# Planned order for SyncE and GpSimd, and a new place for the bf16 parts of the local minima

## Chip, core and metric

One core of a Trainium2 chip runs the kernel. The metric is the device time of one execution in microseconds (us), as the median of several. Engines are named as in the profile: PE is the matrix engine (TensorE) and PEld its weight loads, DVE is VectorE, ACT is ScalarE, POOL is GpSimd, SP is SyncE. SP computes nothing here; it issues nearly all transfers (DMAs), one after the other, and each issue first waits for the semaphores of its source and its destination.

## The reference

From one input x of 4096 rows by 256, two branches are computed on the same layer-normed rows and added to x. The attention branch has 16 heads of 16, whose softmax runs over a rational function of the scores; its projections divide a squared product by a squared distance. The FFN branch is a stack of two layers, each with a local attention (windows of 128 rows that look at themselves and at the window before, 8 heads of 64) and an MLP with a gated GELU of width 682.

```python
def yat_attention(xn, ...):               # S = 4096, H = 16, Dh = 16
    q, k, v = yat_dense(xn, wq, bq, aq), yat_dense(xn, wk, bk, ak), yat_dense(xn, wv, bv, av)
    attn = einsum('bqhd,bkhd->bhqk', q, k)
    sq = attn * attn
    w = sq / (qn + kn - 2.0 * sq + EPS)   # qn, kn: squared norms of q and k
    return softmax(w) @ v @ wo + bo

def layer(x, ...):                        # twice, over all 4096 rows
    q, k, v = split(shift_token(x) @ wqkv)
    q, k = rotary(l2norm(q) * qs, l2norm(k) * ksc)
    x = x + local_attention(q, k, v) @ wo # softmax over 256 keys, with a mask
    a, g = split(layernorm(shift_token(x)) * lg + lb) @ w1 + b1)
    return x + (a * gelu(g)) @ w2 + b2

out = x + yat_attention(layernorm(x)) + layer(layer(layernorm(x)))
```

## The kernel before

A prologue of some 260 us norms the rows, makes q, k and v and stores them in device memory, q and k as three bf16 parts each. Then the main part begins, in which two streams of work are woven into each other.

**The large attention** is cut into 512 tiles: for each of the 16 heads, 32 blocks of 128 queries against all 4096 keys. A tile has two halves of 2048 keys. Per half, PE makes the scores (line L951), ACT squares them (L955), DVE subtracts (`less`, L959). Then a tile is done in one of two ways. Unpaired, each half goes by itself through `positive` (DVE, L972), `log` and `power` (ACT, L978 and L981). Paired, DVE multiplies both halves (`product`, L963), one half goes through the three, and `signed` (DVE, L985) finishes it: less work for ACT, more for DVE. Then `weights` (DVE, L993, twice per tile) makes the softmax's argument and its maximum per query, in `mm`, of which an accumulator read writes the last column. `maximum` (L998 to L1007) turns the maximum of 128 queries into a row of three bf16 parts, `mrow`: SP sends the first part with a DMA (L1004), POOL subtracts it from the maximum (L1007), SP sends the second, POOL subtracts again, SP sends the third. `turn` (PE) first multiplies -1 with that row (L1014), which puts the negated maximum into the bank, and adds the transposed weights (L1017); `exp` (ACT, L1025) and `values` (PE, L1036) follow. After every fourth tile `copied` takes the sum out (ACT, L1043, into `ob`) and SP stores it (L1045).

**The FFN chain** is one long list of steps, written as a generator that yields a step (engine, cost in ns) ahead of each piece of code. Per block of 256 rows and layer (32 in all) it makes q, k, v, and four times `looked` and `summed` (heads in pairs). `looked` makes the scores on PE and the masked, scaled scores with their minimum on DVE (L740, four times, minima in `mx`). Then come the minimum's three bf16 parts: four operations on POOL (L745 to L748, 128x4 each) and three DMAs (L751) into a row `frow`. `summed` uses the row as `turn` does (L760), from a due time of 10,000 ns after the step in which `looked` ended. Then come the MLP of the layer, in 8 blocks of 512 rows (L813 to L915), and `finals`, which adds the attention's result, head half by head half, to the output: `front` (nine DMAs, L1082, L1083, L1087), `middle` (DVE L1095 to L1102; a store `rec` L1097 and a load `pT` L1099 that reads it back), `back` (PE L1108 and L1115, DVE L1110 and L1120). The last block of rows is closed by `last_rows` (L1146 to L1156), after everything else.

**What sets the order.** A planner runs through both streams while the program is built. It keeps one list of ready tasks for PE, ACT, DVE and one called X, which takes no engine; it picks by rank, charges each task its cost, and writes the instructions when a task starts. A task X with no cost is thus a point in planned time, behind the step ahead of it. The chain's steps get a due time in half tiles, from the costs so far (DVE's and ACT's times 0.5, PE's times 1) over the constant CHAIN_NS = 2.5755e6. Whether a tile is paired is decided by which of ACT and DVE has more planned load. For PE, ACT and DVE this planned order is kept as it is; for SP and POOL, a scheduler of the framework decides the order of instructions, from its own estimates and priorities. Every engine works through its list in order, so an instruction that waits holds up all behind it.

Of the kernel before, what the change touches and what calls it, by code (L numbers as in the profile page):

```python
# [182 lines left out]
def plan_all(plan, acts, chain, halves):  # L183
# [32 lines left out]
    def soft(n, m):  # L216
        i, half = divmod(n, 2)
        exps = []
        for z in range(2):
            w = plan.add("PE", 427 + 8 * 109, lambda z=z: acts.turn(n, z), n + RANK["W"] + 0.3 * z, [m], [last["W"]],  # L220
                         takes=[(PS, (n, z, 1))], gives=[(R, n)] if z else [])
            last["W"] = w
            e = plan.add("ACT", 905, lambda z=z: acts.exp(n, z), n + RANK["E"] + 0.3 * z, [w], takes=[(PE2, (n, z))], gives=[(PS, (n, z, 1))])
            exps.append(e)
        fresh = [last["copy"]] if half == 0 and i % 4 == 0 else []
        last["P"] = plan.add("PE", 874, lambda: acts.values(n), n + RANK["P"], exps + fresh, [last["P"]],
                             gives=[(PE2, (n, 0)), (PE2, (n, 1))], mode="C")
        if half and i % 4 == 3:
            last["copy"] = plan.add("ACT", 465, lambda: acts.copied(i), n + RANK["O"], [last["P"]])

# [42 lines left out]
def tile_yat_attention_and_local_ffn(ctx: ExitStack, tc: tile.TileContext, io, out):  # L273
# [322 lines left out]
    def ffn():  # L596
        for l in range(DEPTH):
# [63 lines left out]
            for g in range(NGF):  # L661
# [50 lines left out]
                if g + 1 < NGF:  # L712
                    nxt = fetch(g + 1)
                osum = fa.tile([128, 2, INNER], F32, name="xm2")

                def looked(c):

                    P = fb.tile([128, 2, 2, 256], F32, name="P")
                    mx = fb.tile([128, 4], F32, name="mx")
# [16 lines left out]
                    yield step("DVE", 1620, give=2)  # L736
                    for e in range(2):
                        for b in range(2):
                            mk = msk[:, 0 if (g == 0 and b == 0) else 1]
                            V.tensor_tensor_reduce(P[:, e, b], pss[:, e, b], mk, rn[:, 0, b, 2 * c + e:2 * c + e + 1], 3.0e38,  # L740
                                                   ALU.add, ALU.min, mx[:, 2 * e + b:2 * e + b + 1])
                    yield step("X", 0)
                    m3 = fb.tile([128, 3, 4], BF, name="fm3")
                    md = fb.tile([128, 4], F32, name="fmd")
                    G.tensor_copy(m3[:, 0], mx)  # L745
                    G.tensor_tensor(m3[:, 1], mx, m3[:, 0], ALU.subtract)
                    G.tensor_tensor(md, mx, m3[:, 0], ALU.subtract)
                    G.tensor_tensor(m3[:, 2], md, m3[:, 1], ALU.subtract)  # L748
# [3 lines left out]
                    held[c] = P, mT, plan.now + 10000.0  # L752
# [30 lines left out]
                for c in range(5):  # L783
                    if c < 4:
                        yield from looked(c)
                    if c:
# [17 lines left out]
                V.tensor_tensor(xm, pw, xres, ALU.add)  # L804
                nc.sync.dma_start(xm_d[l][g * GT + 1:(g + 1) * GT + 1].rearrange("(t p) c -> p t c", p=128), xm)
# [23 lines left out]
            for g in range(NG):  # L829
# [16 lines left out]
                if g + 1 < NG:  # L846
                    nxt = shifted(g + 1)
                h2 = []
                for c in range(2):
# [6 lines left out]
                    V.tensor_scalar(h2[c], ph, lngb[:, 0, c:c + 1], lngb[:, 1, c:c + 1], ALU.mult, ALU.add)  # L856
                gg = fa.tile([128, 6, 512], F32, name="kv")
# [38 lines left out]
                if l < DEPTH - 1:  # L896
                    for c in range(2):
# [6 lines left out]
                        V.tensor_copy(xoT, ph)  # L904
                        for z in range(2):
# [3 lines left out]
                else:  # L909
# [4 lines left out]
                    V.tensor_tensor(xo, xo, xin, ALU.add)  # L914
                    nc.sync.dma_start(ff_d[g].rearrange("(t p) c -> p t c", p=128), xo)  # L915
# [7 lines left out]
    class Acts:  # L923
# [11 lines left out]
        def scores(self, n, z):  # L935
            i, half = divmod(n, 2)
            h, qt = tiles[i]
            if half == 0 and z == 0:
# [4 lines left out]
                if qt % 4 == 0 and i // 4 + 1 < len(quads):  # L943
# [96 lines left out]
        def copied(self, i):  # L1040
            h, qt = tiles[i]
            self.ob = hp.tile([128, 512], F32, name="ob", bufs=1)
            A.copy(self.ob, pav)  # L1043
            if i + 1 < len(tiles):
# [120 lines left out]
    with tc.manual_schedule(engines={mybir.EngineType.PE, mybir.EngineType.Activation, mybir.EngineType.DVE}):  # L1165
# [59 lines left out]
```

## Time and profile before

| what | value |
|---|---|
| median of 3 runs | 7330.53 us (7329.86 to 7334.82) |
| the profiled execution | 7328.83 us, its span 7327.0 us |
| granted TensorE clock, mean | 0.981 |
| rows of maxima: POOL L1007, 1024 times | 1033.9 us busy, 1010 ns each |
| parts of the local minima: POOL L745 to L748, 128 times each | 216.9, 203.2, 200.9 and 152.2 us |
| DMA issues of `mrow`, `frow`, Q, `ob` | 1536, 384, 384, 127 |

The span is the time from the first to the last instruction of the profiled execution. "Busy" counts an engine's own instructions; issuing a DMA and waiting are not busy time. A line such as "PE pt L1014 <- DMA mrow<-mm: 108.2, 38, 8.8" reads: PE stood idle ahead of L1014 until a DMA into mrow landed, 108.2 us in all, 38 times, 8.8 at most. In rows of groups the numbers after the bar are busy us and mean ns of one. Rows of a timeline give start, duration, engine, line, operation and tiles, the count, and in brackets the idle time before and what ended it.

### The profile page before, as it was taken

The numbers are of one execution on the slowest core, as the hardware profiler recorded it, in microseconds if no ns is written. First come the engines' busy times: TensorE is split into PE (matmuls) and PEld (weight loads), VectorE is DVE, ScalarE is ACT, GpSimd is POOL, SyncE is SP. The second block draws the span as 40 slices with busy tenths as digits, with TensorE's granted clock in tenths as the row PEclk, the third lists the DMA queues.
The fourth block names the chain that finished last, engine by engine and source line by source line (L and its number), as shares of the span: only waits on it lengthen the run. The fifth ranks groups of instructions, "written<-read, shape, count | busy, mean of one in ns | idle before, by whom it ended". The sixth has DMA issues, their size and how long they took to land. (4 is left out here: it accounts for less than half of the span.)

```text
span 7327.0 us, 158565 instructions
## 1 busy us (share of the span) xinstructions
PE 6747.6 (92%) x66274; PEld 4786.4 (65%) x67136; DVE 6907.5 (94%) x7307; ACT 6972.8 (95%) x6761; POOL 1806.4 (25%) x1567
## 2 busy tenths in 40 slices
PE   7799999999999998899999999999999999999998
PEld 3466666666676665666666676666666666666665
DVE  8999999999999998899999999999999999899998
ACT  8899999999999998899999999999999999899998
POOL 0123233223332322212223322332232220011210
PEclk9899999999999999999999999999999999999999
DMA  3201010010000111011110010101010023101012
GB/s 130 76 16 21 17 24 15 17 22 17 20 19 15 30 40 26 19 31 24 35 21 19 20 19 17 23 14 25 15 23 15 17 59 87 36 21 31 20 46 77
DMA packets 542303, 223.84 MB, mean 31 GB/s; under 512 B 374988, under 2 KB 514003, under 8 KB 539538
## 3 DMA queue, kind: packets, MB, share of 16 engines
q1 hardware_dynamic: 539650, 212.73, 12.3%
q8 instruction: 527, 8.63, 0.5%
q14 instruction: 190, 1.56, 0.1%
q10 hardware_dynamic: 1936, 0.92, 0.0%
HBM read 124.59 MB, written 88.08 MB: 29 GB/s over the span
## 5 line engine op out<-in xcount | busy, mean ns | idle before, releaser
L1017 PE MATMUL pt<-ident,r 128*128 128x128 f32 x16384 | 2497.5, 276 | 0.0
L1017 PEld LDWEIGHTS pt<-ident,r 128*128 128x128 f32 x16384 | 2082.7, 143 | 577.3 <-issue 199.4
L1025 ACT ACTIVATE pe<-pt 128x1024 f32<-128x1024 f32 x2048 | 2178.8, 1099 | 147.0 <-PE pt L1017 122.5
L955 ACT ACTIVATE r<-pt 128x1024 f32<-128x1024 f32 x2048 | 2120.9, 1104 | 86.5 <-PE pt L951 45.0
L1007 POOL TENSOR_TENSOR mm<-mm 128x1 f32<-128x1 f32 x1024 | 1033.9, 1010 | 4714.3 <-DVE mm L993 4547.7
L1014 PE MATMUL pt<-mrow,neg 128*128 128x512 bf16 x4096 | 1577.6, 385 | 220.8 <-DMA mrow<-mm 108.2
L978 ACT ACTIVATE u<-u 128x2048 f32<-128x2048 f32 x702 | 1395.4, 1997 | 26.8 <-DVE u L972 26.4
L981 ACT ACTIVATE u<-u 128x2048 f32<-128x2048 f32 x702 | 1403.5, 1999 | 0.7
L959 DVE TENSOR_SCALAR r<-r 128x2048 f32<-128x2048 f32 x1024 | 1242.5, 1221 | 65.2 <-ACT r L955 64.8
L993 DVE CUSTOM_DVE_ANT_0 r<-r,u,mm 128x2048 f32<-128x2048 f32 x512 | 1201.3, 2346 | 63.4 <-ACT u L981 58.4
L951 PE MATMUL pt<-K,Q 128*128 128x512 bf16 x3234 | 1013.2, 383 | 199.7 <-ACT pe L1025 129.8
L993 DVE CUSTOM_DVE_ANT_0 r<-r,u 128x2048 f32<-128x2048 f32 x512 | 1169.1, 2283 | 13.0 <-ACT u L981 6.4
L1036 PE MATMUL pv<-pe,vh 128*17 128x128 f32 x32768 | 1074.1, 275 | 21.4 <-ACT ob L1043 7.9
L1036 PEld LDWEIGHTS pv<-pe,vh 128*17 128x17 f32 x32768 | 819.0, 97 | 298.7 <-issue 279.7
L985 DVE SCALAR_TENSOR_TENSOR u<-u 128x2048 f32<-128x2048 f32 x322 | 736.1, 2286 | 74.6 <-ACT u L981 73.8
L951 PEld LDWEIGHTS <-Q 128*128 128x128 bf16 x4096 | 375.4, 99 | 574.6 <-issue 393.6
L963 DVE TENSOR_TENSOR u<-r,r 128x2048 f32<-128x2048 f32 x322 | 735.6, 2285 | 1.9
L1014 PEld LDWEIGHTS <-neg 128*128 128x128 bf16 x4096 | 406.7, 99 | 350.7 <-issue 249.6
L972 DVE TENSOR_SCALAR u<-r 128x2048 int32<-128x2048 int32 x380 | 457.1, 1219 | 1.6 <-DMA q_d<-pb 1.5
L972 DVE TENSOR_SCALAR u<-u 128x2048 int32<-128x2048 int32 x322 | 394.4, 1225 | 7.5
L863 PE MATMUL pf<-pT,wqkv_s 128*128 128x512 f32 (+1 forms) x768 | 367.5, 601 | 4.2 <-DVE kv L883 1.5
L745 POOL CAST fm<-mx 128x4 bf16<-128x4 f32 x128 | 216.9, 1695 | 481.2 <-DVE mx L740 470.5
(211 smaller groups left out, 6005.1 us busy)
## 6 DMA issues: line engine op xcount, KB each, us to landing
o<-ob SPq DMA_DIRECT2D x127, 256.0 KB
mrow<-mm SPq DMA_DIRECT2D x1536, 0.2 KB
Q<-q_d SPq DMA_DIRECT2D x256, 48.0 KB
K<-k_d SPq DMA_DIRECT2D x32, 384.0 KB
tab<-in_tables_dram SPq DMA_DIRECT2D x32, 256.0 KB
xres<-xres SPq DMA_DIRECT2D x32, 256.0 KB
xm<-xm SPq DMA_DIRECT2D x32, 256.0 KB
P<-xm SPq DMA_DIRECT2D x32, 256.0 KB
```

The source lines that it names most:

```text
L951: T.matmul(ps[:, j * 512:(j + 1) * 512], lhsT=Q[:, (qt % 4) * 128:(qt % 4 + 1) * 128], rhs=K[:, o + j * 512:o + (j + 1) * 512], start=True ...
L955: A.activation(self.r[n][:, z * 1024:z * 1024 + 1024], self.pt.pop((n, z)), AF.Square)
L959: V.tensor_scalar(self.r[n], self.r[n], 1.0, 1.0e-9, ALU.subtract, ALU.subtract)
L972: V.tensor_scalar(self.part(i, h).bitcast(I32), src.bitcast(I32), 0x7FFFFFFF, None, ALU.bitwise_and)
L978: A.activation(self.part(i, h), self.part(i, h), AF.Ln)
L981: A.activation(self.part(i, h), self.part(i, h), AF.Exp, scale=-2.0)
L993: V.tensor_tensor_reduce(self.r[2 * i + h], self.r[2 * i + h], self.part(i, h), 1.0 if self.paired[i] else -0.5, init, ALU.mult, ALU.max, ...
L1007: G.tensor_tensor(mm[:, c_ + 1:c_ + 2], mm[:, c_:c_ + 1], head[:, 2 * c_ + 1:2 * c_ + 2], ALU.subtract)
L1014: T.matmul(pt[:, 512 * b:512 * b + 512].rearrange("p (s n) -> p s n", s=4), lhsT=neg1, rhs=self.mT[i].unsqueeze(1).broadcast_to([128, 4, 1 ...
L1017: T.matmul(pt[:, 512 * b + j * 128:512 * b + (j + 1) * 128], lhsT=self.r[n][:, o + j * 128:o + (j + 1) * 128], rhs=ident, is_transpose=Tru ...
L1025: A.activation(pe, self.pt.pop((n, z)), AF.Exp)
L1036: T.matmul(pav[32 * (j % 4):32 * (j % 4) + 17, (qt % 4) * 128:(qt % 4) * 128 + 128], lhsT=vh[h % 2][:, kt, :], rhs=pe[:, j * 128:(j + 1) * ...
```

## The change

SP and POOL are added to the engines whose order is the planned one. So that a DMA stands on SP's list behind the planned end of what it reads, X steps are put ahead of several stores, the store of `ob` becomes an X task of its own behind the copy (`stored`), the loads of the next block (`fetch`, `shifted`) move behind later steps, and Q is loaded at the second tile of a quad instead of the first. The three parts of a local minimum are made by three instructions on DVE in the step that makes the minima (cost 2050 instead of 1620): two subtractions of the upper half of the number's bits, seen as bf16, and one cast of all three parts. The local rows' due time is 6,000 ns instead of 10,000. The rows of maxima stay as they were, with POOL's two subtractions.

```diff
--- before.py
+++ after.py
@@ -227,6 +227,7 @@
                              gives=[(PE2, (n, 0)), (PE2, (n, 1))], mode="C")
         if half and i % 4 == 3:
             last["copy"] = plan.add("ACT", 465, lambda: acts.copied(i), n + RANK["O"], [last["P"]])
+            plan.add("X", 0, lambda: acts.stored(i), n, [last["copy"]])
 
     def begin(n):
         sq = []
@@ -709,14 +710,12 @@
                                  start=k == 0, stop=k == 1)
                     yield step("DVE", 600, give=True)
                     V.tensor_copy(va[:, (2 * g + b) % 3, :, 0:FD], pv.rearrange("p (h d) -> p h d", h=FH))
-                if g + 1 < NGF:
-                    nxt = fetch(g + 1)
                 osum = fa.tile([128, 2, INNER], F32, name="xm2")
 
                 def looked(c):
 
                     P = fb.tile([128, 2, 2, 256], F32, name="P")
-                    mx = fb.tile([128, 4], F32, name="mx")
+                    mx = fb.tile([128, 3, 4], F32, name="mx")
 
                     yield step("PE", 1200, "R", take=2)
                     pss = ps_s.tile([128, 2, 2, 256], F32, name=acts.name("pt", "f"))
@@ -733,23 +732,22 @@
                                 else:
                                     T.matmul(pss[:, e, b, j * 128:(j + 1) * 128], lhsT=lq, rhs=kT[r:r + 64, c, (s0, s1)[j]],
                                              start=True, stop=True)
-                    yield step("DVE", 1620, give=2)
+                    yield step("DVE", 2050, give=2)
                     for e in range(2):
                         for b in range(2):
                             mk = msk[:, 0 if (g == 0 and b == 0) else 1]
                             V.tensor_tensor_reduce(P[:, e, b], pss[:, e, b], mk, rn[:, 0, b, 2 * c + e:2 * c + e + 1], 3.0e38,
-                                                   ALU.add, ALU.min, mx[:, 2 * e + b:2 * e + b + 1])
+                                                   ALU.add, ALU.min, mx[:, 0, 2 * e + b:2 * e + b + 1])
+                    m3 = fb.tile([128, 3, 4], BF, name="fm3")
+                    hd = mx.bitcast(BF).rearrange("p j (n w) -> p j n w", w=2)[:, :, :, 1]
+                    for c_ in range(2):
+                        V.tensor_tensor(mx[:, c_ + 1], mx[:, c_], hd[:, c_], ALU.subtract)
+                    V.tensor_copy(m3, hd)
                     yield step("X", 0)
-                    m3 = fb.tile([128, 3, 4], BF, name="fm3")
-                    md = fb.tile([128, 4], F32, name="fmd")
-                    G.tensor_copy(m3[:, 0], mx)
-                    G.tensor_tensor(m3[:, 1], mx, m3[:, 0], ALU.subtract)
-                    G.tensor_tensor(md, mx, m3[:, 0], ALU.subtract)
-                    G.tensor_tensor(m3[:, 2], md, m3[:, 1], ALU.subtract)
                     mT = frow[c % 2]
                     for c_ in range(3):
                         nc.sync.dma_start(mT[c_:c_ + 1], m3[:, c_])
-                    held[c] = P, mT, plan.now + 10000.0
+                    held[c] = P, mT, plan.now + 6000.0
 
                 def summed(c):
                     P, mT, at = held.pop(c)
@@ -783,6 +781,8 @@
                 for c in range(5):
                     if c < 4:
                         yield from looked(c)
+                    if c == 1 and g + 1 < NGF:
+                        nxt = fetch(g + 1)
                     if c:
                         yield from summed(c - 1)
                 oT = fa.tile([128, 4, GT], F32, name="qT")
@@ -802,6 +802,7 @@
                 yield step("DVE", 600, give=True)
                 xm = fa.tile([128, 2, D], F32, name="xm")
                 V.tensor_tensor(xm, pw, xres, ALU.add)
+                yield step("X", 0)
                 nc.sync.dma_start(xm_d[l][g * GT + 1:(g + 1) * GT + 1].rearrange("(t p) c -> p t c", p=128), xm)
 
             if l == DEPTH - 1:
@@ -843,8 +844,6 @@
                 hn = fa.tile([128, 4, D], F32, name="qT")
                 for t in range(4):
                     V.tensor_scalar(hn[:, t], xh[:, t], mv[:, t, 0:1], rstd[:, t:t + 1], ALU.subtract, ALU.mult)
-                if g + 1 < NG:
-                    nxt = shifted(g + 1)
                 h2 = []
                 for c in range(2):
                     yield step("PE", 510, take=True)
@@ -854,6 +853,8 @@
                     yield step("DVE", 725, give=True)
                     h2.append(fb.tile([128, 512], F32, name="pT"))
                     V.tensor_scalar(h2[c], ph, lngb[:, 0, c:c + 1], lngb[:, 1, c:c + 1], ALU.mult, ALU.add)
+                if g + 1 < NG:
+                    nxt = shifted(g + 1)
                 gg = fa.tile([128, 6, 512], F32, name="kv")
 
                 def up(s_, m):
@@ -902,6 +903,7 @@
                         yield step("DVE", 600, give=True)
                         xoT = fb.tile([128, 512], F32, name="pT")
                         V.tensor_copy(xoT, ph)
+                        yield step("X", 0)
                         for z in range(2):
                             nc.sync.dma_start(xT_d[l + 1][2 * g + z][c * 128:(c + 1) * 128], xoT[:, z * GT:(z + 1) * GT])
                     for z in range(2):
@@ -912,6 +914,7 @@
                     nc.sync.dma_start(xin, acc_d[g].rearrange("(t p) c -> p t c", p=128))
                     yield step("DVE", 1135)
                     V.tensor_tensor(xo, xo, xin, ALU.add)
+                    yield step("X", 0)
                     nc.sync.dma_start(ff_d[g].rearrange("(t p) c -> p t c", p=128), xo)
 
 
@@ -940,7 +943,7 @@
                     assert self.valued >= 8 * NT * h
                     load_k(h + 1)
                     load_v(h + 1)
-                if qt % 4 == 0 and i // 4 + 1 < len(quads):
+                if qt % 4 == 1 and i // 4 + 1 < len(quads):
                     load_q(*quads[i // 4 + 1])
             if z == 0:
                 self.r[n] = hr.tile([128, 2048], F32, name=self.name("r", n))
@@ -1041,6 +1044,9 @@
             h, qt = tiles[i]
             self.ob = hp.tile([128, 512], F32, name="ob", bufs=1)
             A.copy(self.ob, pav)
+
+        def stored(self, i):
+            h, qt = tiles[i]
             if i + 1 < len(tiles):
                 nc.sync.dma_start(o_d[qt // 4][h], self.ob)
                 if h == H - 1:
@@ -1162,7 +1168,7 @@
 
     plan = Plan()
     acts = Acts()
-    with tc.manual_schedule(engines={mybir.EngineType.PE, mybir.EngineType.Activation, mybir.EngineType.DVE}):
+    with tc.manual_schedule(engines={mybir.EngineType.PE, mybir.EngineType.Activation, mybir.EngineType.DVE, mybir.EngineType.SP, mybir.EngineType.Pool}):
         plan_all(plan, acts, chain(), 2 * len(tiles))
         last_rows(acts.ob)
```

## The prediction

> **What bounds the kernel now.** I read the page first: part 1 for the load of each engine, then the waits, then busy time by stretches of 200 us, then the timeline around one stall and around the end.
>
> ```profile
> span 7327.0 us, 158565 instructions
> PE 6747.6 (92%) x66274; PEld 4786.4 (65%) x67136; DVE 6907.5 (94%) x7307; ACT 6972.8 (95%) x6761; POOL 1806.4 (25%) x1567
> ```
>
> Three engines are nearly full. What is left to gain is idle time of ACT, 7327.0 - 6972.8 = 354 us, and of DVE, 420 us. The second view shows where ACT's idle time lies:
>
> ```profile
> 800.00:1000.00 200.00, 190.41 (x1991) 140.38 (x2012) 195.97 (x228) 198.64 (x197) 70.67 (x62) 1.00 0.08 15
> 1000.00:1200.00 200.00, 185.26 (x1884) 136.26 (x1906) 187.74 (x196) 190.45 (x192) 46.70 (x44) 0.98 0.12 24
> sum 4400.00, PE 4117.56 PEld 3028.53 DVE 4245.33 ACT 4312.75 POOL 1271.97; mean PE 187.16 PEld 137.66 DVE 192.97 ACT 196.03 POOL 57.82
> ```
>
> The columns after the stretch are PE, PEld, DVE, ACT and POOL busy. The sum is over 22 stretches, 400 to 2600 and 3800 to 6000 us, in which the FFN's local attention runs beside the large attention. ACT is idle for 4400.00 - 4312.75 = 87 us there, very unevenly: 1.4 us in a quiet stretch, 9.6 in the next one. The eleven quietest of the 22 lose 1.5 us each. At that rate all would lose 33, so 54 us are stalls. The waits name them:
>
> ```profile
> PE pt L1014 <- DMA mrow<-mm: 108.2, 38, 8.8
> PEld L1014 <- DMA mrow<-mm: 44.7, 15, 9.3
> ACT pe L1025 <- PE pt L1017: 122.5, 105, 9.9
> ```
>
> PE waits 153 us for the row of maxima, and ACT then waits for PE. Asked by stretch, 33.7 of the 153 fall between 400 and 2600 us and 30.9 between 3720 and 6000; 52.5 lie from 2600 to 3720, in the FFN's MLP. One stall in order of time, first POOL's rows, then SP's and PE's:
>
> ```profile
> 1126.93 2.24 POOL L745 CAST fm<-mx 128x4 bf16<-128x4 f32 x1 [10.67 <-DVE mx L740]
> 1129.25 1.08 POOL L746 TENSOR_TENSOR fm<-mx,fm 128x4 bf16<-128x4 f32 x1
> 1130.29 2.25 POOL L747 TENSOR_TENSOR fmd<-mx,fm 128x4 f32<-128x4 f32 x1
> 1132.61 1.06 POOL L748 TENSOR_TENSOR fm<-fmd,fm 128x4 bf16<-128x4 f32 x1
> 1133.62 3.39 POOL L1007 TENSOR_TENSOR mm<-mm 128x1 f32<-128x1 f32 x2
> ...
> 1129.20 4.96 SPq L751 DMA_DIRECT2D frow<-fm  x3
> 1134.26 3.24 SPq L1004 DMA_DIRECT2D mrow<-mm  x3
> 1140.22 0.59 PE L1014 MATMUL pt<-mrow,neg 128*128 128x512 bf16 x1 [3.53 <-DMA mrow<-mm]
> ```
>
> The maximum was ready at 1129.13 (the end of its read on DVE at 1129.05). Its row was sent at 1134.26, since POOL was still on the four operations for the local minima and SP stood in front of their transfers. PE lost 3.5 us. So in the attention stretches a good part of the 54 us comes from what the change removes.
>
> **The change, part by part.** *POOL's four operations per local tile go* (L745 to L748, 128 times; means 1.695, 1.587, 1.570 and 1.189 us, 6.04 together). POOL then has only the 1024 subtractions of L1007. Upper bound of the gain: all 54 us of stalls, with SP's order below. Lower bound: 0, if the rows stay late for another reason. L1007 alone runs from 189 to 11197 ns, and its longest lie in the MLP, which this part does not touch. I take 54 in the attention stretches and nothing in the MLP's 52.5.
>
> The trace first: 6.04 us for four operations of 128x4 on POOL stand against 0.155 us for one such operation on DVE (L402, median), ten times as long for each. The Trainium skill (GPSIMD Engine Reference, Key points) says that for elementwise work the DVE is structurally about 2x faster. By that rule the four would hold POOL for 1.2 us, a fifth of what is measured, the gain would be about 11 us, and the sum below would come out some 43 us later, slower than before. The trace decides here.
>
> *DVE gets three tiny operations per local tile*: two subtractions of 128x4 (0.155 each, row L402) and a cast of 128x12, which the trace has not; the nearest are 0.166 (L404, 128x4) and 0.169 (L703, 128x16), from below 0.081 (the read of an accumulator). 128 x (2 x 0.155 + 0.166) = 61 us, bounds 31 and 65.
>
> *The planner answers.* It charges DVE 430 ns more per local tile and so picks fewer paired tiles. In the built programs 316 tiles of 512 are paired instead of 322. Each of the six takes 2.286 + 2.285 + 1.225 - 2 x 1.219 = 3.36 us from DVE and gives ACT one Ln and one Exp of 128x2048, whose starts lie 1.80 us apart when they follow each other (2880.09 and 2881.89). So DVE: 61 - 20 = +41 us; ACT: 12 x 1.80 = +22 us. ACT is the fuller engine (196.03 against 192.97 of 200 in the stretches above), and DVE's 7 us idle in each 200, some 3.5%, cover its 41 us (0.6%). I take 22; without that cover it is 22 + 41 = 63.
>
> *SP and POOL in the planned order.* In front of the rows, SP now waits for many things:
>
> ```profile
> SPq L751 <- POOL fm L745: 433.7, 116, 15.0
> SPq L1045 <- ACT ob L1043: 249.0, 67, 10.1
> SPq L338 <- PE pt L951: 227.6, 62, 11.2
> SPq L638 <- DVE qr L647: 103.3, 23, 9.8
> ```
>
> The change moves each of these behind the event that frees it: Q by one tile, the fetch of hT and tab behind two local blocks, `ob` behind its copy, the local minima's transfers behind DVE. Their gain is inside the 54. What strict order adds: in the final rows, `rec` and `pT` now stand together, so SP waits for the store to land (1.74 us between the two issues at 7290.81 and 7292.55), and the front's nine transfers go in one piece (0.61 us each, 5.5 together), where before rows of maxima were let in between. 16 finals x 7.2 us = 115 us of SP held; a tile's row comes every 13.7 us (L1007 runs from 262.9 to 7297.8 us for 512 tiles), so 8 or 9 rows meet it and are late by half, 31 us. That is the upper bound; 0 is the lower. About one turn in ten waits for its row today (53 waits, 512 tiles), one in five would when it is this late: 6 us.
>
> The local minima's transfers themselves are due 6.0 us after the planner's step instead of 10.0. Three issues at 0.48 and the landing fit; if another triple stands in front, L760 waits a little. I see no such wait in the trace now and price it at nothing, up to 3 us; what hides it is PE's other work, 8% idle.
>
> *The FFN chain runs later.* Its pace is the sum of step costs times 0.5 for DVE, over CHAIN_NS = 2.5755e6, and that constant stays. 128 x 430 x 0.5 = 27,520 is 1.07% of it, 5.5 of 512 tiles. The built programs agree: the FFN's last matmuls stand after the turns of 502 tiles instead of 496. The eight final blocks then no longer fit beside the attention: after the last `weights` on DVE before there is one `back` (L1110, L1120 twice), after the change one `back` and three `middle` and `back` pairs. The end in the trace:
>
> ```profile
> 7289.63 0.57 DVE L1095 TENSOR_REDUCE msk<-hT 64x64 f32<-64x256 f32 x1
> 7290.81 0.49 SPq L1097 DMA_DIRECT2D rec<-msk  x1
> 7297.36 0.08 DVE L993 DVE_READ_ACCUMULATOR2_ANT mm<- 128x1 f32 x1
> 7312.12 1.89 PE L1146 MATMUL pt<-ob,consts 128*16 128x512 f32 x4 [0.71 <-ACT ob L1043]
> ```
>
> From the last weights (7297.4) to the end is 29.6 us, 14.9 of them from L1146 on. After the change: one `back` 4.5 (7300.54 to 7305.05); from one `middle` to the next 1.2 to `rec`, 1.7 to `pT`, eight loads 4.9 and 4.8 from the last issue to L1095, 12.6, twice; from the last `middle` to its last matmul some 10 (4.9 of them from 7299.38 to 7304.3); 14.9: 54.6, which is 25 more. Against that, DVE stood idle from 7282.8 to 7289.63 for the last front, and did that `middle` (3 us), ahead of the last weights; both go, 10 us. And 12 us of other vector work of the finals leave the time ahead of the last weights; half of it counts, as ACT is beside it. 25 - 10 - 6 = +9. Bounds: -5 (all of it counts and the loads are quicker) and +36 (nothing comes earlier and three finals take 15.4 each, as 7289.63 to 7305.05).
>
> **Sum.** The profiled execution took 7328.8 us, its span 7327.0 and 1.8 around it. -54 + 22 + 6 + 9 = -17: 7312 by its own time. The median of the runs shown is 7330.5, 1.7 above; so 7313 to 7314, and I say 7313. What a measurement can tell from no change is about 0.2%, 15 us, so the forecast is a small gain just beyond that.
>
> **Rivals.** *Half of the stalls stay.* The subtractions of L1007 remain on POOL and are themselves held up (3.39 us for two in the stall shown). If only 27 of the 54 go, the time is 7340, no change. For it: the same kind of wait in the MLP with no local minima at all. Against: in the stall shown both the work in front of it and SP's order go.
>
> *The vector work lands on the path whole* (slower). Place: the three operations stand between the local minima and the next `weights` or `less`. The chain alternates between DVE and ACT (DVE L993 waits 64.9 us for ACT L981 and ACT L978 26.4 for DVE L972), so a time added on each may add up: 63 in place of 22, 7354. It decides once DVE's idle time in the attention stretches is under the 41 us put in, when stalls that let it catch up are gone; today it is 155 us there (4400.00 - 4245.33), which is against it.
>
> *The end is drawn out.* The tail at its upper bound, +36 in place of +9: 7340. It alone makes the kernel slower only if the rest gains under 21.
>
> *It does not do what it says*, if the order were as before: the built programs show otherwise, POOL's instructions are 512 fewer and the stores stand later on SP.
>
> **How the numbers follow.** Forecast 0.44. Half of the stalls 0.17, drawn-out end 0.12, vector work on the path 0.27. The middle two lie within 0.2%, a little of the last of them beyond; so faster 0.44, same 0.25, slower 0.31. The likeliest one's own range is 7290 to 7325. For the whole: down to 7274, where 87 us of idle time fall nearly whole and the end costs nothing; up to 7358, the vector rival with a few us of new waits.
>
> **What would show it.** POOL busy falls from 1806 by about 773 us (128 x 6.04). PE's waits for mrow in 400 to 2600 and 3720 to 6000 fall from 65 us to under 20, and in 2600 to 3720 stay near 50. ACT's busy time is about 22 us higher and the stretches of 200 us lose 1 to 3 us each. SP no longer waits for `fm`, and less than 100 us for `ob`. The last weights come about 55 us ahead of the end. Wrong if the rows are still late in the attention stretches, if SP waits for `ob` or `pT` with rows behind it, or if DVE's idle time there shrinks to nothing.

## The result, and the profile after the change

The changed kernel takes 7402.82 us (median of 4 runs, 7399.35 to 7409.95) against 7332.67 us for the kernel before in the same comparison: a ratio of 1.0095, 95% interval 1.0078 to 1.0113. It is slower by 70 us; 7313 was forecast, and the range ended at 7358. The profiled execution took 7402.08 us.

The page of the changed kernel, first lines and part 1:

```profile
span 7400.3 us, 158075 instructions
PE 6759.9 (91%) x66278; PEld 4785.5 (65%) x67136; DVE 6943.1 (94%) x7685; ACT 6993.4 (95%) x6773; POOL 1042.7 (14%) x1055
```

Busy times moved as forecast: POOL 1806.4 to 1042.7, ACT 20.6 more, DVE 35.6 more. The span grew by 73.3 us, of which ACT's growth can be at most 21; the rest is new idle time. The same three rows of the waits (engine, line, what released it; us in all, times, longest):

```profile
ACT pe L1028 <- PE pt L1020: 126.2, 126, 13.6
PE pt L1017 <- DMA mrow<-mm: 107.3, 38, 9.9
...
PEld L1017 <- DMA mrow<-mm: 55.5, 17, 7.3
```

(L1017 and L1020 are L1014 and L1017 of before, three lines further down.) PE waits for the row of maxima as long as before, 107 against 108 us, but in another place. PE's row alone, asked by stretch:

| PE waits for `mrow`, us | 400 to 2600 and 3720 to 6000 | 2600 to 3720 | from 6000 on |
|---|---|---|---|
| before | 21.8 + 26.8 | 35.1 | 14.7 |
| after | 2.5 + 6.9 | 32.3 | 62.8 |

In the attention stretches the stalls nearly went; in the finals they came back. The busy time of the 22 stretches, asked as two, says the same (columns PE, PEld, DVE, ACT, POOL):

```profile
sum 4400.00, PE 4112.13 PEld 3020.66 DVE 4288.41 ACT 4349.93 POOL 583.06; mean PE 2056.06 PEld 1510.33 DVE 2144.21 ACT 2174.96 POOL 291.53
```

ACT's idle time there is 50 us, from 87. To follow the loss through the span, I take the time at which a tile's last `weights` ends and compare it with the same tile of before:

| us, after minus before | tile 128 | 210 | 420 | 440 | 500 | 511 | end of span |
|---|---|---|---|---|---|---|---|
| after | -14.6 | -24.4 | -23.8 | +4.5 | +19.8 | +32.8 | +73.3 |

The change is 24 us ahead when the first finals begin (tile 420), loses 57 in and between the finals, and 40 more behind the last `weights`, which come 70.0 us ahead of the end instead of 29.6. The first loss in the timeline of the changed kernel (start, duration, engine, line, operation):

```profile
6063.53 0.39 SPq L1129 DMA_DIRECT2D acc<-qT  x1
6065.63 0.59 DVE L1101 TENSOR_REDUCE msk<-hT 64x64 f32<-64x256 f32 x1
...
6066.82 0.49 SPq L1103 DMA_DIRECT2D rec<-msk  x1
...
6069.23 0.30 SPq L1105 DMA_DIRECT2D pT<-rec  x1
6069.57 0.65 SPq L1088 DMA_DIRECT2D fsq<-o  x1
...
6073.06 0.08 DVE L996 DVE_READ_ACCUMULATOR2_ANT mm<- 128x1 f32 x1
...
6074.95 0.47 SPq L1093 DMA_DIRECT2D qT<-in_L_attn_inputs_q_dram  x1
6075.54 2.02 SPq L1007 DMA_DIRECT2D mrow<-mm  x3
...
6084.83 0.59 PE L1017 MATMUL pt<-mrow,neg 128*128 128x512 bf16 x1 [4.52 <-DMA mrow<-mm]
```

From 6063.53 to 6075.42 SP issues a store, `rec`, `pT` and nine loads and no row of maxima. The maximum was complete at 6073.14; its first part goes out 2.4 us late, and the third lands 9.2 us after that issue, where 5.9 is usual in the trace of before; nine loads were issued ahead of it. PE loses 4.5 us. Of the 28 tiles 418 to 431 and 497 to 510, 11 have a first part more than 1 us late, and 2 before the change.

### The profile page after: what moved, and what is told of

The parts are those of the page before. It is cut to its first block, busy times and chain, and to the rows that moved or that the text cites. A ratio compares the mean times of both kernels' runs of the same rounds, so it can differ in the third digit from the quotient of the medians.

```text
span 7400.3 us, 158075 instructions
## 1 busy us (share of the span) xinstructions
PE 6759.9 (91%) x66278; PEld 4785.5 (65%) x67136; DVE 6943.1 (94%) x7685; ACT 6993.4 (95%) x6773; POOL 1042.7 (14%) x1055
## 5 line engine op out<-in xcount | busy, mean ns | idle before, releaser
L1020 PE MATMUL pt<-ident,r 128*128 128x128 f32 x16384 | 2492.6, 275 | 0.0
L1020 PEld LDWEIGHTS pt<-ident,r 128*128 128x128 f32 x16384 | 2078.9, 143 | 560.8 <-issue 180.5
L1028 ACT ACTIVATE pe<-pt 128x1024 f32<-128x1024 f32 x2048 | 2208.7, 1115 | 165.5 <-PE pt L1020 126.2
L958 ACT ACTIVATE r<-pt 128x1024 f32<-128x1024 f32 x2048 | 2144.4, 1118 | 89.7 <-remote 43.4
L1017 PE MATMUL pt<-mrow,neg 128*128 128x512 bf16 x4096 | 1575.5, 385 | 219.9 <-DMA mrow<-mm 107.3
L981 ACT ACTIVATE u<-u 128x2048 f32<-128x2048 f32 x708 | 1418.2, 2012 | 31.2 <-DVE u L975 30.6
L984 ACT ACTIVATE u<-u 128x2048 f32<-128x2048 f32 x708 | 1427.6, 2017 | 0.7
L1017 PEld LDWEIGHTS <-neg 128*128 128x128 bf16 x4096 | 406.4, 99 | 348.3 <-issue 229.8
L975 DVE TENSOR_SCALAR u<-r 128x2048 int32<-128x2048 int32 x392 | 472.2, 1219 | 1.6 <-DMA q_d<-pb 1.5
L677 PE MATMUL pf<-wqkv_s,hT 128*128 128x512 f32 x512 | 247.7, 606 | 10.7 <-DMA hT<-xT 5.9
```

The costliest lines, as they stand in the source:

```text
L958: A.activation(self.r[n][:, z * 1024:z * 1024 + 1024], self.pt.pop((n, z)), AF.Square)
L975: V.tensor_scalar(self.part(i, h).bitcast(I32), src.bitcast(I32), 0x7FFFFFFF, None, ALU.bitwise_and)
L981: A.activation(self.part(i, h), self.part(i, h), AF.Ln)
L984: A.activation(self.part(i, h), self.part(i, h), AF.Exp, scale=-2.0)
L1017: T.matmul(pt[:, 512 * b:512 * b + 512].rearrange("p (s n) -> p s n", s=4), lhsT=neg1, rhs=self.mT[i].unsqueeze(1).broadcast_to([128, 4, 1 ...
L1020: T.matmul(pt[:, 512 * b + j * 128:512 * b + (j + 1) * 128], lhsT=self.r[n][:, o + j * 128:o + (j + 1) * 128], rhs=ident, is_transpose=Tru ...
```

## The experiments

All are shown in one table, as comparisons with the kernel before run on the same chip. "At 416" and "at 511" are the shifts against before of the table above, in the profiled execution; "tail" is the time from the last `weights` to the end.

| kernel | median us | ratio, 95% interval | at 416 | at 511 | tail | PE waits for `mrow` from 6000 on |
|---|---|---|---|---|---|---|
| before | 7331.8 to 7333.7 | 1 | 0 | 0 | 29.6 | 14.7 |
| after | 7402.82 | 1.0095 (1.0078 to 1.0113) | -20.7 | +32.8 | 70.0 | 62.8 |
| chain_on_time | 7365.92 | 1.0042 (1.0027 to 1.0057) | -32.4 | +24.7 | 35.7 | 84.6 |
| before_chain_late | 7398.33 | 1.0080 (1.0063 to 1.0097) | +15.4 | +31.1 | 67.7 | 27.2 |
| sp_scheduled | 7332.43 | 0.9998 (0.9989 to 1.0008) | -37.1 | -31.5 | 65.5 | 23.1 |
| both_mended | 7334.54 | 1.0001 (0.9991 to 1.0010) | -24.2 | -3.9 | 40.0 | 35.7 |
| sp_scheduled_on_time | 7310.23 | 0.9967 (0.9955 to 0.9979) | -31.2 | -23.8 | 35.2 | 32.4 |
| dve_parts_alone | 7313.91 | 0.9971 (0.9959 to 0.9982) | -26.4 | -20.1 | 35.2 | 32.1 |
| order_alone | 7468.39 | 1.0182 (1.0168 to 1.0196) | +71.7 | +141.2 | 33.5 | 70.5 |
| front_in_pairs | 7354.81 | 1.0029 (1.0020 to 1.0039) | -26.2 | +12.9 | 35.7 | 58.2 |
| rec_later | 7319.32 | 0.9979 (0.9969 to 0.9988) | -18.6 | -0.9 | 33.3 | 33.2 |

One caution on the shifts: chain_on_time, front_in_pairs, rec_later and both_mended differ in the finals alone, yet stand between -18.6 and -32.4 at tile 416. Single profiled executions differ by 14 us up to there; smaller differences of shifts mean nothing. Nor is a profiled execution always near the median: that of rec_later took 7331.66 us, the longest of its ten, and that of chain_on_time 7359.68, the shortest of its four. And a shift compares two kernels only where their chains stand alike: before_chain_late, which has nothing of the change but the lateness, is 26.6 us ahead at tile 210 as well, and loses it again later.

**The tail: is it the late chain?** chain_on_time is the changed kernel with the chain's pace put back by 1.07%, the share that the dearer local step added:

```diff
-CHAIN_NS = 2.5755e6
+CHAIN_NS = 2.603e6
```

> The changed kernel with CHAIN_NS = 2.603e6 instead of 2.5755e6, so that the FFN chain is back at its old place beside the attention (its last matmuls behind 496.8 of 512 tiles, before 496.2, after the change 501.8). Theory A (the chain is late): from the last weights to the end falls from 70 us to about 35, the time to about 7365. Theory B (it is SP's strict order that draws the end out): the end stays at 60 to 70 us, the time within 10 us of 7402.

before_chain_late does the reverse to the kernel before and leaves all else:

```diff
-CHAIN_NS = 2.5755e6
+CHAIN_NS = 2.548e6
```

> The kernel before with CHAIN_NS = 2.548e6, nothing else: its chain is as late as the changed kernel's (501.5 of 512 tiles). Theory A: the end grows from 30 to some 60 us and the time to 7355 to 7370. Theory B: the end stays under 40 us, the time under 7340.

The tail falls from 70.0 to 35.7 us in the one and rises from 29.6 to 67.7 in the other; the kernels move by 37 us down and 67 up. So the late chain costs some 34 to 38 us at the end, with and without everything else of the change (30 in the pair with SP scheduled, below). Of the rest of the 67, 27 arise between tiles 260 (-6.5) and 300 (+20.6), early in the second layer; what does this was not tried and stays open. Whether the late chain gains something before the end can't be told: the last `weights` come at 7330.3 in the changed kernel and at 7322.1 with the chain on time, but at 7266.0 and 7273.6 in the pair with SP scheduled, and both differences are within the 14 us.

**SP's order.** sp_scheduled leaves SP to the framework's scheduler, as before the change, and keeps everything else:

```diff
-    with tc.manual_schedule(engines={mybir.EngineType.PE, ..., mybir.EngineType.SP, mybir.EngineType.Pool}):
+    with tc.manual_schedule(engines={mybir.EngineType.PE, ..., mybir.EngineType.Pool}):
```

> The changed kernel with SP's order left to the framework's scheduler as before; POOL, DVE and the planner as in the changed kernel. Theory B: tiles 420 to 440 (28 us lost) and 500 to 511 (13 us lost) come back, the attention stretches lose a part of the 37 us of ACT idle time that went; about 7375. Theory A alone: the end stays near 70 us, tiles 420 to 440 too, and the time is 7400 to 7420.

From tile 420 to 511 the changed kernel loses 57 us (from -23.8 to +32.8), this one 9 (from -40.3 to -31.5), and its tail is still long, 65.5. So the strict order of SP is what loses in the finals, and the tail is a loss of its own. The pair with the chain on time says the same: chain_on_time loses 56 us there, sp_scheduled_on_time 10. The median of 7332.43 is 43 us under what theory B gave; of the 69 us between the two spans, 48 fall in the finals, 16 ahead of tile 420, which is near the noise, and 5 in the tail. Against my expectation of the attention stretches, SP's planned order brought nothing there: with it the shifts at tile 416 are -18.6 to -32.4, without it -26.4 to -37.1.

Both causes taken out together, with the parts on DVE and POOL's planned order kept, is sp_scheduled with CHAIN_NS = 2.603e6:

> The changed kernel with SP left to the framework's scheduler, and CHAIN_NS 2.603e6 in place of 2.5755e6, so that the chain ends as early as before the change. Theory (the tail and SP's strict order in the finals are two separate losses): the tail falls from 65 us after the last weights to about 33, as it fell from 70 to 36 when only CHAIN_NS was changed; the last weights stay near 31 us ahead of before's. So 7332 - 30 = about 7302, faster than before by 0.4%. Rival (the late chain was also what gave the 31 us, since work moved behind the last weights): the tail falls by 32 and the last weights come later by as much, 7330.

7310.23 us, 0.33% faster than before: the two losses are separate, and the tail's gain (65.5 to 35.2) is kept, less 8 us by which the last `weights` come later. The theory's 7302 was 8 too low. In its finals the scheduler lets a row into the front's loads:

```profile
6012.87 1.22 SPq L1089 DMA_DIRECT2D P<-o  x2
6015.06 2.79 SPq L1007 DMA_DIRECT2D mrow<-mm  x3
6017.91 0.63 SPq L1089 DMA_DIRECT2D P<-o  x1
```

**Which part gains?** dve_parts_alone is the kernel before with the three instructions on DVE, their cost and due time, and nothing else of the change, SP and POOL both scheduled, and the chain on time (in part):

```diff
-CHAIN_NS = 2.5755e6
+CHAIN_NS = 2.603e6
-                    yield step("DVE", 1620, give=2)
+                    yield step("DVE", 2050, give=2)
+                    m3 = fb.tile([128, 3, 4], BF, name="fm3")
+                    hd = mx.bitcast(BF).rearrange("p j (n w) -> p j n w", w=2)[:, :, :, 1]
+                    for c_ in range(2):
+                        V.tensor_tensor(mx[:, c_ + 1], mx[:, c_], hd[:, c_], ALU.subtract)
+                    V.tensor_copy(m3, hd)
                     yield step("X", 0)
-                    G.tensor_copy(m3[:, 0], mx)
...
-                    held[c] = P, mT, plan.now + 10000.0
+                    held[c] = P, mT, plan.now + 6000.0
```

> The kernel before with nothing but the local minima's parts made on DVE (three operations, cost 2050, due time 6,000) and CHAIN_NS 2.603e6; SP and POOL both left to the scheduler, loads and stores where they were. Theory (POOL's work ahead of the rows of maxima was what cost the attention stretches): as sp_scheduled_on_time within 10 us, about 7300 to 7310, and PE's waits for mrow in 400 to 2600 and 3720 to 6000 us fall from 65 to under 25. Rival (the planned order of POOL and the later loads and stores are what helped): no gain in those stretches, 7325 to 7345.

7313.91 us; its interval overlaps that of sp_scheduled_on_time almost wholly, and PE waits 16.1 us for `mrow` in the attention stretches, under the 25 of the theory. So the gain of the change comes from this edit; POOL's planned order and the later loads and stores add nothing that these runs can tell. The chain's constant, which the edit changes too, is not what cuts the stalls: ACT's idle time in the 22 stretches is 50 to 61 us in all eight kernels with the parts on DVE, under either constant, and 87, 112 and 130 in the three with the parts on POOL (before, before_chain_late, order_alone). The due time of 6,000 ns goes with the parts on DVE in all eight, so its share is not shown.

order_alone is the opposite half: the changed kernel with the four operations back on POOL (cost 1620, due time 10,000) and CHAIN_NS as it was.

```diff
-                    yield step("DVE", 2050, give=2)
+                    yield step("DVE", 1620, give=2)
...
+                    G.tensor_copy(m3[:, 0], mx)
+                    G.tensor_tensor(m3[:, 1], mx, m3[:, 0], ALU.subtract)
+                    G.tensor_tensor(md, mx, m3[:, 0], ALU.subtract)
+                    G.tensor_tensor(m3[:, 2], md, m3[:, 1], ALU.subtract)
-                    held[c] = P, mT, plan.now + 6000.0
+                    held[c] = P, mT, plan.now + 10000.0
```

> The changed kernel with the local minima's four operations put back on POOL (cost 1620, due time 10,000): only the order of SP and POOL and the places of loads and stores are changed; CHAIN_NS is 2.5755e6 as before, and the chain's pace is thus as before. Theory (strict order of SP costs in the finals and gains little in the attention stretches; the tail is set by the chain's pace): tail about 30 to 36; the finals lose about 50 us against before as in the changed kernel; the attention stretches gain at most 10: 7365 to 7390. Rival (the order is worth as much as the parts on DVE): 24 us gained up to tile 420, then 50 lost: 7350 to 7360.

7468.39 us, beyond either expectation: the order, with the moved loads and stores, costs 1.8% by itself. The finals lose 61 us (from +80.6 at tile 420 to +141.2), as in the changed kernel, and the tail is short, 33.5, as the theory said; but up to tile 420, where I expected a small gain, it loses 81, some 23 of them between tiles 160 and 260, in the MLP. In the attention stretches PE waits 41.1 and 52.5 us for `mrow`, against 21.8 and 26.8 before. One of these stalls, in the timeline of order_alone:

```profile
1682.27 13.37 SPq L750 DMA_DIRECT2D frow<-fm  x5
...
1691.67 0.08 DVE L997 DVE_READ_ACCUMULATOR2_ANT mm<- 128x1 f32 x1
1691.76 1.19 POOL L746 TENSOR_TENSOR fmd<-mx,fm 128x4 f32<-128x4 f32 x1
...
1693.03 2.12 POOL L747 TENSOR_TENSOR fm<-fmd,fm 128x4 bf16<-128x4 f32 x1
...
1695.74 0.54 SPq L632 DMA_DIRECT2D hT<-xT  x1
...
1697.80 7.51 SPq L1008 DMA_DIRECT2D mrow<-mm  x6
...
1704.01 0.59 PE L1018 MATMUL pt<-mrow,neg 128*128 128x512 bf16 x1 [5.52 <-DMA mrow<-mm]
```

The maximum is complete at 1691.75. SP stands in the planned place of the local minima's transfers and waits for POOL's parts until 1695.6, then issues the moved `fetch`, and only at 1697.80 the row. The planned time holds no cost for POOL's operations, so a DMA that follows them in the plan stands on SP's list too early, and strict order makes every later one pay. How much of the 81 us comes this way, and how much from POOL's own planned order, was not tried.

**What of SP's order in the finals?** both_mended is chain_on_time with two edits: the front's nine transfers go in pairs with planned time between them, and `rec` stands behind the planned end of `middle` instead of its start, with `pT` 2 us of planned time later. front_in_pairs has the first alone, rec_later the second. Due times behind a moved transfer are shortened by about as much (8000 to 4500 and 4000 to 2500 in the first edit).

```diff
             for s_ in range(4):
+                if s_:
+                    yield step("X", 1250)
                 nc.sync.dma_start(d4[0:w // 2, s_], ...)
                 nc.sync.dma_start(s4[s_ // 2][0:w, s_ % 2], ...)
```

```diff
-            nc.sync.dma_start(rec_d[c][g][0:w // 16]..., dn[0:w // 2])
             de = fb.tile([8, 512], F32, name="pT")
-            nc.sync.dma_start(de[0:w // 16], rec_d[c][g][0:w // 16])
             V.tensor_tensor(s4[0][0:w], s4[0][0:w], s4[1][0:w], ALU.add)
             on = fa.tile([128, 512], F32, name=("xm", "xres")[k % 2])
             V.tensor_tensor(on[0:w], s4[0][0:w, 0], s4[0][0:w, 1], ALU.add)
-            return g, w, fin, last, de, on, plan.now + 8000.0
+            yield step("X", 2000)
+            nc.sync.dma_start(rec_d[c][g][0:w // 16]..., dn[0:w // 2])
+            yield step("X", 0)
+            nc.sync.dma_start(de[0:w // 16], rec_d[c][g][0:w // 16])
+            return g, w, fin, last, de, on, plan.now + 3500.0
```

> The changed kernel with CHAIN_NS = 2.603e6, and in the final rows the nine transfers of front issued in pairs with 1.25 us of planned time between them, rec behind the planned end of middle and pT 2 us later, each as a step of its own, so that rows of maxima can stand between. If A and B are both right: the end about 35 us, tiles 420 to 440 and 500 to 511 lose under 10 us instead of 41, the time 7320 to 7340. If only A: 7360 to 7370. If only B: 7370 to 7380.

> chain_on_time (the changed kernel, CHAIN_NS 2.603e6) with one more edit: the front's nine transfers are issued in pairs, with 1250 ns of planned time between pairs, so that the rows of maxima can stand between them; rec and pT are left together. From tile 420 to 511 chain_on_time loses 56 us against before, and both_mended, which has both edits, 23. Theory (the front in one piece makes the rows late): most of the 33 us come back here, 7335 to 7347. Rival (SP held by rec and pT does it): nothing comes back, 7360 to 7372.

> chain_on_time with the other edit alone: rec is stored behind the planned end of the middle and pT loaded right behind it at a later due time of the back, while the front's nine transfers stay in one piece. Theory (the front in one piece makes the rows late): little comes back of the 33 us, 7355 to 7370. Rival (rec and pT): most comes back, 7335 to 7347.

both_mended lies in its range, though it still loses 23 us from tile 420 to 511 (from -27.2 to -3.9) where under 10 was expected. My theory for the other two fell. The front in pairs brings 11 us at most (7365.92 to 7354.81, with intervals that overlap); `rec` later brings 47 (to 7319.32), and the rival was right. Rows more than 1 us late among the 28 tiles: 11 in chain_on_time, 12 in front_in_pairs, 3 in rec_later and in both_mended. SP in rec_later:

```profile
6032.31 0.50 SPq L1108 DMA_DIRECT2D rec<-msk  x1
6034.84 0.30 SPq L1110 DMA_DIRECT2D pT<-rec  x1
6035.23 2.98 SPq L1007 DMA_DIRECT2D mrow<-mm  x3
6038.26 0.67 SPq L1088 DMA_DIRECT2D hT<-o  x1
```

It is not SP's wait itself that went. From 6000 us on it waits longer between `rec` and `pT` (35.5 us in 15 waits, against 21.1 in 14 in chain_on_time) and less ahead of `rec` for the DVE work that makes it (16.5 against 31.6): 52 and 53 us together. What changed is the neighbourhood. In the rows above a row of maxima stands between `pT` and the front, where the stall of the changed kernel has store, `rec`, `pT` and nine loads in one piece of 12 us. Places where `rec`, `pT` and the front's eight loads from `o` follow each other with no row between them, up to the last `weights`, number 2 in the kernel before, 8 in the changed one, 13 in chain_on_time, 6 in rec_later, and 2 or 3 in the kernels with SP scheduled. Their number is not the whole of it, since both_mended has 8 as well. The edit moves the next front too, by its 2000 ns, so the runs show that this edit pays; that it pays by breaking up the piece is likely, but not shown. That both edits together (7334.54) are slower than one (7319.32) is not explained.

## Why the prediction was wrong, step by step

**Right.** *POOL's operations*: 773 us less were forecast, 764 measured. *DVE's three operations*: 61 us forecast, 41.5 + 22.2 = 64 measured. *ACT*: 22 forecast, 20.6 measured, and DVE's idle time in the attention stretches (155 to 112 us) covered its part, so the rival of the vector work on the path whole did not occur. *The MLP's* waits stayed, 35.1 to 32.3. *The cause of the stalls*: POOL's work and what waited for it, shown by dve_parts_alone and by ACT's idle time in the eleven kernels, but for the share of the due time. PE's waits for `mrow` in the attention stretches fell from 48.6 to 9.4 us.

**Right in kind, too large.** *The 54 us of stalls*: ACT's idle time in the attention stretches fell by 37, between the forecast and the rival in which half stays. A smaller flaw stands in its reading: PE's and PEld's waits were added to 153 us, but they name the same stalls (chain_on_time has both at 6038.6, 4.7 and 4.4 us); PE's 108 alone is the number. The 54 did not rest on it; the "53 waits" in the term of the finals did, and are 38.

**Right only by its partner.** "SP and POOL in the planned order", counted as part of the 54, is worth nothing beside the parts on DVE, and without them it loses 81 us up to tile 420. That SP would no longer wait for `fm`, and under 100 us for `ob`, was wrong too, as its own waits in the changed kernel show:

```profile
SPq L749 <- DVE fm L745: 505.5, 123, 11.8
SPq L1051 <- ACT ob L1046: 390.4, 73, 16.1
...
SPq L1103 <- DVE msk L1102: 37.9, 16, 5.4
...
SPq L1105 <- DMA rec<-msk: 28.3, 16, 3.9
```

It waits 390 us for `ob`, from 249, and 505 for `fm`, from 831. An X step behind a task puts a store behind the task's planned end; the task's real end is later. With the same X steps and SP scheduled, the wait for `ob` is 231 (sp_scheduled).

**Wrong: "SP's strict order in the finals, 6 us".** This term is 48 us instead (57 lost with it, 9 without it in sp_scheduled). That `rec`, `pT` and the front hold up rows was right, and so about were the "8 or 9 rows" (12 late by over 1 us in the changed kernel, between tiles 423 and 433 and between 502 and 510). Wrong was the price of one: "one in five waits" by half of 7.2 us. The piece is 10 to 12 us long and not 7.2, because `rec` stands in the same step as the DVE work that makes it, so SP also waits for that work (37.9 us), and the store of the `back` before stands in front of it; moving `rec` and `pT` alone brings 47 us back (rec_later). Then the row is issued behind the loads, and its third part lands 9 to 13.5 us after the maximum in the late tiles of the first group and 9 to 19 in those of the last, against 6 to 7 on the mean before.

**Wrong: "the end, +9 us".** It is +40. The mechanism (three `middle` and `back` pairs behind the last `weights`) was right, and so is the rival "the end is drawn out", whose +36 it nearly equals. The tail in the changed kernel:

```profile
7330.18 0.08 DVE L996 DVE_READ_ACCUMULATOR2_ANT mm<- 128x1 f32 x1
...
7338.74 0.58 PE L1017 MATMUL pt<-mrow,neg 128*128 128x512 bf16 x1 [5.75 <-DMA mrow<-mm]
...
7342.60 0.69 DVE L1126 TENSOR_TENSOR qT<-qT,pf 128x512 f32<-128x512 f32 x1 [8.89 <-PE pf L1121]
7343.21 0.58 DVE L1101 TENSOR_REDUCE msk<-hT 64x64 f32<-64x256 f32 x1
...
7359.27 0.57 DVE L1101 TENSOR_REDUCE msk<-fsq 56x64 f32<-56x256 f32 x1
...
7372.42 0.57 DVE L1101 TENSOR_REDUCE msk<-hT 64x64 f32<-64x256 f32 x1
...
7385.54 0.41 SPq L1131 DMA_DIRECT2D out_dram<-xm  x1
```

Against 54.6 us forecast, 70: the first `back` ends 13.0 us behind the last `weights` instead of 4.5, since its second product stands on PE behind a turn that waits for its row; the steps from `middle` to `middle` 16.1 and 13.2 instead of 12.6 each; the last `middle` to its last product 13.1 instead of 10. That is 15 us. The other 16 are the credits, "10" and "6", for DVE work that leaves the time ahead of the last `weights`. They are not seen: with the chain on time the last `weights` come 8 us earlier in one pair of kernels and 8 later in the other, against 16 later by the credits. Why is not shown; the time that DVE gave up need not lie on the path, as ACT was nearly as full ahead of the last `weights` (from 7100 to 7297 us before the change, ACT is idle for 12.5 us and DVE for 10.3).

By its own terms the sum is thus -37 + 20 (ACT) for the attention, 48 for SP, 40 for the tail: +71, and 73 is the change of span. The agreement is closer than its parts: by the shifts, the three are -24, +57 and +40. Had the chain's constant been moved with the step's cost, and SP left alone, a small gain would have come out: sp_scheduled_on_time has 7310, and 7313 was predicted. That the number comes so near is partly luck, since ACT's idle time in the attention stretches falls by 26 us there, not by 54.

## What to carry to other kernels

Where an engine's queue is put into a planned order, no instruction in it is issued ahead of one that the plan puts before it, so each wait for something the plan doesn't cost (POOL's work, a store's landing, a step's own result) holds up all behind it; look for the longest piece of the queue in which no urgent transfer stands, and price that piece whole, with the slower landing of what follows it. When a step's cost is raised, the constants that pace other work by the sum of costs must be raised with it. And split a change into its parts before it is judged: here one part gained 20 us, and the other two, the strict order of SP and the late chain, took back 90.

## What was not expected of the hardware

**POOL's short operations are slow only beside some work of DVE.** The prediction put 6.04 us of POOL against 0.155 us for one operation on DVE and took POOL to be ten times slower. In order_alone the same operation is seen at 0.19 us and at 1.2 to 2.2:

```profile
4943.56 0.48 DVE L739 CUSTOM_DVE_ANT_0 P<-pt,msk,rn 128x256 f32<-128x256 f32 x1
4943.65 0.19 POOL L746 TENSOR_TENSOR fmd<-mx,fm 128x4 f32<-128x4 f32 x1
...
4946.31 2.35 DVE L997 CUSTOM_DVE_ANT_0 r<-r,u,mm 128x2048 f32<-128x2048 f32 x1
4946.52 2.20 POOL L745 TENSOR_TENSOR fm<-mx,fm 128x4 bf16<-128x4 f32 x1
...
4948.58 1.23 DVE L963 TENSOR_SCALAR r<-r 128x2048 f32<-128x2048 f32 x1
4948.67 1.19 POOL L746 TENSOR_TENSOR fmd<-mx,fm 128x4 f32<-128x4 f32 x1
```

Beside `weights` (2.35 us) and a 128x2048 scaling (1.23 us) POOL's operation ends when DVE's does; beside the local minima, whose source `pt` is in PSUM, the matrix engine's output memory, it takes 0.19. Over the whole trace of order_alone the 128x4 operations take 0.20 us in the median beside the local minima (37 of them) and with DVE idle (19), and 2.2 beside `weights` (150). The Trainium skill (SBUF — State Buffer, section "SBUF: two separate sides") says that DVE and GpSimd share one pair of ports of SBUF, the on-chip memory of all other operands here, and that a GpSimd operation and a DVE operation that uses both of DVE's ports or reads two inputs from SBUF exclude each other for a whole instruction. These rows agree. So by these rows the gain of the parts on DVE is hardly that DVE is faster at them (0.16 against 0.19, neither ten times nor twice as fast), but that they no longer wait for DVE's long instructions.

**The clock falls in a drawn-out tail.** Two stretches of 20 us, of the changed kernel and of chain_on_time (PE, PEld, DVE, ACT, POOL busy; then PEclk, the granted clock):

```profile
7360.00:7380.00 20.00, 8.34 (x13) 3.43 (x13) 7.89 (x11) 0.00 (x0) 0.00 (x0) 0.56 0.36 111
```

```profile
7320.00:7340.00 20.00, 15.41 (x147) 12.24 (x148) 6.33 (x8) 7.17 (x7) 0.39 (x2) 0.83 0.06 10
```

With PE idle for most of the stretch the clock is 0.56, and one product of L1121 takes up to 0.80 us, where its median in the 400 us ahead of the tail is 0.38. A group of four products of a `back` then takes 2.07 us instead of 1.13, and the pair ahead of it (L1114) 2.04 instead of the 1.12 at 7352.30, in rows of the changed kernel:

```profile
7357.50 1.13 PE L1121 MATMUL pf<-fwo_s,xres 128*128 128x256 f32 x4
...
7377.04 2.04 PE L1114 MATMUL pf<-pT,qr 8*128 8x512 f32 x2 [5.27 <-DMA pT<-rec]
...
7379.86 2.07 PE L1121 MATMUL pf<-fwo_s,xres 128*128 128x256 f32 x4 [0.78 <-DVE xres L1116]
...
7382.72 2.07 PE L1121 MATMUL pf<-fwo_s,xres 128*128 128x256 f32 x4 [0.78 <-DVE xm L1126]
```

In the last `back` nothing else runs beside its pair and two groups, so an estimate from these rows puts 2.8 of the 3.1 us by which "the last `middle` to its last product" was mis-sized down to the clock. The two groups before (7366.84 and 7369.70) count for less: the next `middle` also needs its loads, the last of them issued at 7367.16, and by the 4.8 us from there to L1095 that the prediction read, it could hardly have begun ahead of 7372.0, against 7372.42. The Trainium skill (TensorE: Matmul & The Clock Gate, "Part 1: The HAM clock gate") states that an idle array is clocked at half rate and gets its full rate back only after some microseconds of sustained work; the 0.56 of this tail, with PE busy for 8.34 of 20 us in short groups, agrees.
